# All transposes of a norm-and-convolution kernel on VectorE and DMA, sums on GpSimd, and the order from a list scheduler

## The chip, the cores and the metric

The kernel runs on one core of one Trainium2 chip. The metric is the device time of one execution in microseconds; the time of before is the median of three executions. Every tensor is fp32.

## The reference

Two layers run on x of shape (4, 128, 128, 128): 4 images, 128 channels, 128x128 positions. Cut to what matters:

```python
def _block(x, ...):                                  # tokens = positions, 128 channels each
    t = x.reshape(b, c, h * w).transpose(0, 2, 1)
    t = _ln(t, ln0_g, ln0_b)
    y1 = _ln(t, ln1_g, ln1_b)
    t = t + einsum('btc,oc->bto', sigmoid(y1) * y1, W_out)
    y2 = _ln(t, ln2_g, ln2_b)
    wht = einsum('btc,oc->bto', y2, W_whiten)
    k = square(relu(einsum('btc,hc->bth', wht, W_key)))      # 512 hidden
    kv = einsum('bth,ch->btc', k, W_value)
    r = sigmoid(einsum('btc,oc->bto', wht, W_recep))
    return (t + r * kv).transpose(0, 2, 1).reshape(b, c, h, w)

# layer 0: _gn is a group norm over 4 channels and all positions of an image.
# out1 is _block(inp); out2 is _block on the image with h and w swapped, swapped back.
# _block works on each token alone, so out1 == out2.
x = x + (out1 + out2)(_gn(x))
# layer 1: 3x3 convolution of _gn(x), 128 to 128 channels, a bias, and a gate per channel
x = x + (conv(_gn(x)) + bias) * sigmoid(relu(avg @ se_w1.T) @ se_w2.T)
```

The group norm needs the sums of a whole image before its first token can be worked on. So the convolution of an image can start only when layer 0 of that image has ended.

## The kernel before, in words

**Tiling.** An image has 16384 positions: 8 blocks of 16 rows, or 16 pairs `g` of two chunks `h` of 512 tokens. Layer 0 goes by pairs, the convolution by blocks. Channel layout means 128 channels on the partitions and tokens along the row; token layout means 128 tokens on the partitions and, along the row, four groups of 128 channels.

**Layer 0.** Each step has a short name, which the orders use:

- `u` (`lay`, ACT) applies the group norm in channel layout. `Tu` (`lay_turned`) turns the chunk to token layout by four TensorE transposes through `turned` at L659. `bn0` (DVE, L692) takes the token statistics.
- `nb` (`norm_terms`) makes `rs` and `nb` of a layer norm: small operations on POOL (L704, L705, L722) and a power of -1/2 (L717, POOL).
- `t` (`scaled`, ACT, L666) normalizes; `g` and `b` (POOL, L739, L743) apply gain and shift; `bn1`, `nb`; `z` (ACT, L666) normalizes again; `Tz` turns `z` back to channel layout on TensorE.
- `silu` (ACT), `att` (TensorE, L760) returns to token layout, `T` (DVE, L764) adds it to `t`. `bn2` and `nb2` make the last norm, whose 1/std per token is turned by DVE (`rc`, L772), stored to HBM (`W`, L778, four DMAs) and read back broadcast over the partitions as `R` (L783, two DMAs).
- `tt` turns `t` to channel layout on TensorE. `cp` (DVE, L796) multiplies it with `R` into the input `y2` of the keys; `S` (DVE, L844) adds twice `tt` to x.
- `pk` (4 matmuls, L807), `re` and `sq` (ACT, L811, L817), `kv` (4 matmuls, L834), `pr` (L825), `th` (ACT), `q` (DVE, L850), `x1` (POOL, L854), and `bx`, the statistics for layer 1 (DVE, L860).

**Convolution.** Per block, six products `m0` to `m5` (Winograd along the rows, four output rows from six inputs) of three accumulating matmuls each (L872 to L874), 12 DVE operations ahead of them (`p`, `q`, `v1`...) and 10 after (`a`, `b`, `y0`...), and two ACT evictions. The x of a block stays in SBUF from layer 0 to the end of its convolution (`xp`, 12 buffers of 1 MB).

**Order.** Every engine works in program order. The program order is written out in text lists: `FILL`, `FIRST`, `HANDOVER`, `ORDER`, `BOUND`, `END`. The convolution of image b lies between the pairs of image b+1; the last image's stands at the end. All DMAs of the main part are issued by SP's queue, in that order too. PSUM has eight banks: `h` 2, `kv` 1, `tr` 2, `ut` 2, `conv` 1.

Of the kernel before, what the change touches and what calls it, by code (L numbers as in the profile page):

```python
# [21 lines left out]
LAG = 4  # L22


ORDER = """
    u1:0 Tu1:0 u0:0 x11:3 Tz10:1 Tu0:0 bn01:0 bn00:0 z11:1 bx1:3 v1:1 pr0:2 Tz11:1 q2:1
    silu0:1 p2:1 re00:2 sq00:2 y2:1 ca:1 att0:1 silu1:1 c0:1 pk01:2 nb0:0 d8:1 kv00:2 T0:1
    y0:1 th0:2 t1:0 bn20:1 v3:1 tt1:2 g1:0 re01:2 in0:0 c1:1 cp1:2 e1:1 att1:1 pk02:2 c3:1
    T1:1 bn21:1 pk10:2 c5:1 b1:0 y3:1 re02:2 S1:2 t0:0 nb2:1 e3:1 pk03:2 v2:1 g0:0 b0:0
    re10:2 c2:1 in1:0 a:1 pk12:2 sq01:2 sq10:2 v0a:1 sq02:2 re03:2 sq03:2 re12:2 b:1 kv01:2  # L30
    kv02:2 rc:1 pk13:2 re13:2 v4:1 pk11:2 kv03:2 sq12:2 c4:0 bn11:0 v5a:0 tt0:1 bn10:0 v0b:1
    pr1:2 q0:2 c:0 d:0 re11:2 sq11:2 S0:1 sq13:2 kv10:2 v5b:0 kv11:2 th1:2 kv12:2 kv13:2
    nb1:0 W:1 y1:0 R0:1 z10:0 q:0 cp0:1 pk00:1 R1:1 x10:2 p:0 bx0:2 q1:2
"""


FILL = """
    fetch:16 u1:0 u0:0 Tu1:0 bn01:0 u0:1 Tu0:0 u1:1 bn00:0 sa0:0 in1:16 pw0:0 in0:16
    fetch:17 nb0:0 t1:0 t0:0 Tu0:1 g1:0 bn00:1 b1:0 u1:2 Tu1:1 in1:17 g0:0 u0:2 in0:17
    bn11:0 fetch:18 b0:0 bn01:1 sa0:1 bn10:0 pw0:1 sa1:0 nb0:1 pw1:0 in1:18 t0:1 in0:18  # L40
    nb1:0 fetch:19 t1:1 Tu1:2 g0:1 bn01:2 b0:1 z10:0 Tu0:2 bn00:2 g1:1 z11:0 Tz10:0 b1:1
    in0:19 silu0:0 Tz11:0 bn10:1 nb0:2 u0:3 att0:0 in1:19 silu1:0 bn11:1 fetch:20 u1:3
    att1:0 sa1:1 T0:0 bn20:0 pw1:1 t0:2 T1:0 t1:2 bn21:0 g0:2 sa2:0 Tu0:3 nb1:1 pw2:0 Tu1:3
    in1:20 u1:4 in0:20 z10:1 g1:2 bn00:3 fetch:21 z11:1 bn01:3 nb2:0 b0:2 Tz10:1 rc:0 nb0:3
    W:0 silu0:1 Tz11:1 att0:1 silu1:1 in1:21 bn10:2 R0:0 att1:1 in0:21 b1:2 t0:3 T0:1
    fetch:22 T1:1 tt0:0 t1:3 g0:3 bn11:2 R1:0 tt1:0 Tu1:4 nb1:2 cp0:0 u0:4 bn20:1 u0:5 Tu0:4
    pk02:0 in1:22 S1:0 u1:5 bn01:4 pk00:0 re02:0 pk01:0 re00:0 g1:3 cp1:0 pk03:0 z10:2
    sq00:0 b1:3 bn00:4 pk11:0 re01:0 b0:3 re03:0 pr0:0 in0:22 z11:2 bn21:1 fetch:23 kv00:0
    nb0:4 pk10:0 S0:0 sq01:0 bn10:3 Tz10:2 re11:0 kv01:0 silu0:2 sa2:1 pk12:0 re10:0 bn11:3
    att0:2 sq02:0 pw2:1 sq03:0 kv02:0 T0:2 th0:0 nb2:1 nb1:3 Tz11:2 t1:4 rc:1 kv03:0 sq10:0  # L50
    W:1 pk13:0 q0:0 silu1:2 Tu1:5 in0:23 re12:0 att1:2 bn20:2 t0:4 R0:1 pr1:0 g1:4 bn01:5
    kv10:0 sq11:0 R1:1 x10:0 T1:2 Tu0:5 sq12:0 kv11:0 z10:3 bn00:5 tt1:1 tt0:1 nb0:5 kv12:0
    th1:0 cp0:1 re13:0 pr0:1 sq13:0 cp1:1 pk03:1 z11:3 S1:1 pk00:1 bn21:2 th0:1 kv13:0 g0:4
    S0:1 re00:1 Tz11:3 bx0:0 pk01:1 re03:1 b1:4 sq00:1 silu1:3 pk02:1 b0:4 bn11:4 re01:1
    Tz10:3 att1:3 re02:1 nb2:2 bn10:4 silu0:3 pk12:1 q1:0 pk10:1 re12:1 T1:3 att0:3 sq03:1
    bn21:3 sq01:1 kv00:1 nb1:4 re10:1 pk11:1 sq02:1 rc:2 sq10:1 W:2 pk13:1 re11:1 T0:3
    kv01:1 sq11:1 bn20:3 t1:5 kv02:1 x11:0 R0:2 kv03:1 sq12:1 nb2:3 tt0:2 q0:1 re13:1 R1:2
    pr1:1 bx1:0 t0:5 kv10:1 S0:2 kv11:1 sq13:1 kv12:1 x10:1 z10:4 cp0:2 tt1:2 pk01:2 g0:5
    S1:2 th1:1 pk00:2 cp1:2 re01:2 g1:5 pk03:2 re00:2 rc:3 kv13:1 sq00:2 re03:2 in1:23
    pk02:2 q1:1 pk10:2 bx0:1 x11:1 kv00:2 Tz10:4 bx1:1  # L60
"""
FILL_SLOTS = 6

EARLY = 2

FIRST = """
    u1:0 u0:0 Tu1:0 pk11:4 re02:4 pr0:4 z11:2 Tu0:0 in1:0 re10:4 silu0:2 Tz11:2 sq01:4
    bn01:0 W:3 att0:2 b1:1 sq10:4 bn00:0 R0:3 T0:2 th0:4 silu1:2 re11:4 kv01:4 b0:1 pk12:4
    sq03:4 tt0:3 bn10:1 sq02:4 pk13:4 sq11:4 cp0:3 re12:4 pr1:4 att1:2 th1:4 kv02:4 re13:4
    kv03:4 nb0:0 bn11:1 bn20:2 T1:2 S0:3 pk01:3 pk00:3 pk03:3 bn21:2 tt1:3 t0:0 q0:4 kv10:4  # L70
    nb1:1 sq12:4 kv11:4 re01:3 re00:3 sq13:4 in0:0 nb2:2 S1:3 kv12:4 sq00:3 kv13:4 R1:3
    x10:4 cp1:3 pk02:3 rc:2 q1:4 bx0:4 t1:0 x11:4 g1:0 z10:1 bx1:4 pk10:3 kv00:3 Tz10:1 g0:0
    re03:3
"""
FIRST_SLOTS = 17

ORDER_FROM = 23
HANDOVER = """  # L80
    load load load fetch:32 sq01:13 W:14 z11:15 re02:13 Tz11:15 R0:14 silu0:15 kv01:13 u1:17
    att0:15 R1:14 silu1:15 b0:16 pk11:13 T0:15 re10:13 att1:15 bn20:15 b1:16 u0:17 pk13:13
    re11:13 T1:15 Tu1:17 * bn21:15 tt0:14 re13:13 pr1:13 sq03:13 sq10:13 nb2:15 pr0:13
    sq02:13 bn01:17 u1:18 Tu0:17 pk12:13 bn00:17 sq11:13 kv02:13 th0:13 bn10:16 nb0:17
    sq13:13 tt1:14 kv03:13 th1:13 cp0:14 re12:13 q0:13 pk00:14 u0:18 bn11:16 kv10:13 sq12:13
    re00:14 pk01:14 cp1:14 x10:13 t1:17 S1:14 kv11:13 sq00:14 pk03:14 nb1:16 S0:14 t0:17
    Tu1:18 kv12:13 re01:14 pk12:14 bn01:18 re03:14 Tu0:18 u0:19 pk02:14 bn00:18 g0:17
    kv13:13 z10:16 rc:15 W:15 g1:17 tt0:15 q1:13 pk10:14 sq03:14 S0:15 sq01:14 nb0:18
    kv00:14 * re12:14 kv01:14 * re02:14 R0:15 * re10:14 pr0:14 bx0:13 sq02:14 R1:15 sq10:14
    pk11:14 sq12:14 Tz10:16 th0:14 b0:17 kv02:14 t1:18 kv03:14 x11:13 cp0:15 pk13:14 re11:14  # L90
    bn10:17 b1:17 t0:18 pk00:15 q0:14 pr1:14 bn11:17 sq11:14 x10:14 Tu0:19 * tt1:15 kv10:14
    * * nb1:17 th1:14 * kv11:14 re00:15 * kv12:14 cp1:15 re13:14 bn00:19 silu0:16 pk02:15
    sq13:14 sq00:15 re02:15 kv13:14 g0:18 S1:15 u1:19 pr1:15 q1:14 z11:16 b0:18 att0:16
    bx0:14 pk01:15 x11:14 z10:17 Tu1:19 Tz11:16 g1:18 bn01:19 pk03:15 th1:15 silu1:16
    kv00:15 T0:16 nb0:19 re01:15 bn20:16 pr0:15 z11:17 att1:16 bn10:18 re03:15 in1:32
    Tz11:17 pk10:15 sq01:15 T1:16 b1:18 sq03:15 bn21:16 Tz10:17 kv01:15 re10:15 nb2:16
    sq02:15 sq10:15 pk11:15 silu1:17 bx1:14 kv02:15 th0:15 kv03:15 silu0:17 t0:19 q0:15
    att0:17 rc:16 x10:15 bn11:18 W:16 pk12:15 re11:15 bx1:13 tt0:16 nb1:18 sq11:15 pk13:15
    T0:17 u0:20 bx0:15 t1:19 R0:16 Tu0:20 bn20:17 kv10:15 kv11:15 R1:16 re12:15 S0:16
    re13:15 att1:17 bn00:20 g0:19 sq12:15 sq13:15 kv12:15 g1:19 * kv13:15 cp0:16 u1:20 *  # L100
    b1:19 u1:21 Tu1:20 q1:15 pk01:16 z10:18 bn01:20 x11:15 pk00:16 nb0:20 re01:16 bx1:15
    Tz10:18 pr0:16 re00:16 T1:17 sq00:16 * tt1:16 silu0:18 bn21:17 * th0:16 att0:18 sq01:16
    cp1:16 nb2:17 t0:20 * pk10:16 p:0 bn11:19 pk11:16 t1:20 pk03:16 S1:16 * T0:18 b0:19
    re10:16 kv00:16 * rc:17 re03:16 in0:32 kv01:16 W:17 g1:20 re11:16 bn10:19 Tu1:21 z11:18
    pk02:16 b1:20 bn01:21 pk12:16 R0:17 re02:16 nb1:19 * Tz11:18 bn11:20 sq02:16 tt0:17
    u0:21 kv02:16 fetch:33 S0:17 sq03:16 bn20:18 * Tu0:21 re12:16 R1:17 pk13:16 * sq10:16
    bn00:21 kv03:16 g0:20 silu1:18 cp0:17 pr1:16 z11:19 q0:16 b0:20 att1:18 sq11:16 kv10:16
    * T1:18 sq12:16 nb0:21 tt1:17 * in0:33 re13:16 kv11:16 in1:33 th1:16 pk00:17 S1:17
    fetch:34 sq13:16 * z10:19 kv12:16 * bn10:20 * * re00:17 kv13:16 bn21:18 nb1:20 * Tz10:19
    * t0:21 cp1:17 pk01:17 in0:34 Tz11:19 pk02:17 re01:17 * * silu1:19 pk10:17 * q:0  # L110
    silu0:19 nb2:18 pr0:17 q2:0 sq00:17 att1:19 * re10:17 att0:19 t1:21 T1:19 pk03:17 q1:16
    x10:16 sq01:17 kv00:17 rc:18 bn21:19 re02:17 W:18 g1:21 kv01:17 sq02:17 T0:19 pk12:17
    th0:17 g0:21 in1:34 re03:17 kv02:17 bn20:19 x11:16 R0:18 sq03:17 tt0:18 z10:20 pk11:17
    S0:18 b0:21 kv03:17 * bx0:16 sq10:17 pk13:17 nb2:19 q0:17 re12:17 Tz10:20 * re11:17
    kv10:17 z11:20 cp0:18 pr1:17 * pk00:18 * sq11:17 b1:21 bn10:21 Tz11:20 re13:17 kv11:17
    silu0:20 p2:0 pk02:18 re00:18 v3:0 silu1:20 pk01:18 v1:0 th1:17 rc:19 att1:20 bn11:21
    W:19 re02:18 att0:20 * re01:18 nb1:21 T1:20 c1:0 sq01:18 bn21:20 u0:22 R1:19 T0:20 u1:22
    bn20:20 R0:19 tt0:19 e1:0 Tu1:22 tt1:18 x10:17 sq02:18 bn01:22 c3:0 R1:18 z11:21 nb2:20
    * fetch:35 sq13:17 sq12:17 Tu0:22 pr0:18 sq00:18 bn00:22 e3:0 pk03:18 th0:18 v4:0 nb0:22
# [17 lines left out]
"""  # L137

BOUND_SLOTS = 1, 7
BOUND = """
# [138 lines left out]
def conv_preact_kernel(  # L282
# [17 lines left out]
    se_w2_t: bass.AP,  # L300
    out: bass.AP,
):

# [876 lines left out]
```

## Time and profile before

| What | Value |
|---|---|
| median of 3 runs | 1856.72 us (1855.88 to 1857.11) |
| profiled execution, own time | 1858.43 us |
| its span, first to last instruction | 1856.7 us |
| busy: PE, DVE, ACT, POOL | 97%, 70%, 68%, 53% of the span |
| moved by DMA | 133.44 MB, mean 72 GB/s |
| mean granted TensorE clock | 0.997 |

A page of the profile lists busy time by engine, the chain of work that ended last (followed back from the last instruction, each step to what released it), and groups of instructions with their mean duration and the idle time ahead of them. An fp32 matmul shows as two records, so 512 matmuls are "x1024". The trace can be asked further: for windows of time, for waits by releaser, and for the chain in order of time.

### The profile page before, as it was taken

What the parts mean: (1) busy time and instruction counts of PE and PEld (TensorE: products, weight loads), DVE (VectorE), ACT (ScalarE), POOL (GpSimd) and SP (SyncE); (2) the same over time, 40 slices, a digit from 0 to 9 for tenths busy, and PEclk for the clock granted to TensorE, in tenths of its full rate; (3) what the DMA queues carried; (4) which work ended last, traced back from release to release, by engine and by line L of the source; (5) the groups of instructions that cost most, each with busy time, mean ns of one, the idle gap of its engine ahead of it and who ended that gap; (6) DMA issues with size and microseconds to landing.
All of it is one profiled execution on the core that took longest, in us unless ns stands there. A gap on an engine that the chain in (4) does not pass through costs nothing.

```text
span 1856.7 us, 20165 instructions
## 1 busy us (share of the span) xinstructions
PE 1801.5 (97%) x6096; PEld 944.4 (51%) x6096; DVE 1308.8 (70%) x2540; ACT 1271.1 (68%) x2493; POOL 989.1 (53%) x1047
## 2 busy tenths in 40 slices
PE   3899999999999999999999999999999999999999
PEld 2555555555445555555555555555555555544443
DVE  6766666676667667877667667877766666666987
ACT  2988998898567777777667767777766777753000
POOL 2867677775355555765435555666445556531111
PEclk9999999999999999999999999999999999999999
DMA  6211112121211222222112212211201211111112
GB/s 231 80 58 46 58 65 99 45 71 58 97 57 63 91 79 95 90 80 104 35 68 92 91 48 67 76 63 69 82 16 65 68 58 69 50 40 46 50 68 90
DMA packets 46057, 133.44 MB, mean 72 GB/s; under 512 B 8679, under 2 KB 15102, under 8 KB 38014
## 3 DMA queue, kind: packets, MB, share of 16 engines
q1 hardware_dynamic: 45504, 131.77, 20.6%
q8 instruction: 48, 0.79, 0.2%
q14 instruction: 59, 0.48, 0.1%
q10 hardware_dynamic: 446, 0.40, 0.1%
HBM read 97.14 MB, written 35.00 MB: 71 GB/s over the span
## 4 chain that ended last, share of the span: by engine, by line
PE 89%; DVE 3%; DMA 1%; ACT 1%; POOL 1%; issue 0%; SPq 0%; DVEq 0%; POOLq 0%
PE kv L834 22%; PE pk L807 22%; PE m L872 9%; PE m L873 9%; PE m L874 8%; PE att L760 6%; PE pr L825 6%; PE tt L659 3%; PE z1t L659 3%; PE ut L659 3%; DMA R<-rd 1%; DMA rd<-rrow 1%; DVE v L896 0%; DVE u L606 0%; SPq L778 0%
## 5 line engine op out<-in xcount | busy, mean ns | idle before, releaser
L811 ACT ACTIVATE h<-pk,kbias 128x512 f32<-128x512 f32 x512 | 349.4, 687 | 234.3 <-PE pk L807 223.2
L807 PE MATMUL pk<-y,wk_s 128*128 128x512 f32 x1024 | 502.1, 593 | 2.2 <-DVE y L796 1.2
L834 PE MATMUL kv<-h,wv 128*128 128x512 f32 x1024 | 492.6, 593 | 0.0
L854 POOL TENSOR_TENSOR x<-x,r 128x512 f32<-128x512 f32 x128 | 167.9, 1312 | 275.9 <-DVE r L850 266.0
L834 PEld LDWEIGHTS kv<-h,wv 128*128 128x128 f32 x1024 | 187.1, 190 | 201.8 <-issue 176.0
L817 ACT ACTIVATE h<-h 128x512 f32<-128x512 f32 x480 | 286.5, 629 | 3.4
L807 PEld LDWEIGHTS pk<-y,wk_s 128*128 128x128 f32 x1024 | 183.7, 190 | 183.1 <-issue 153.7
L717 POOL TENSOR_TENSOR rs<-rs,nhalf 128x8 f32<-128x8 f32 x128 | 226.4, 1769 | 4.3 <-DVE nb L705 4.1
L739 POOL TENSOR_TENSOR t<-t,g 128x512 f32<-128x512 f32 x128 | 163.7, 1284 | 101.3 <-ACT t L666 100.9
L666 ACT ACTIVATE t<-ut,nb,rs 128x128 f32<-128x128 f32 x512 | 191.3, 466 | 37.0 <-POOL nb L722 31.2
L666 ACT ACTIVATE z<-t,nb,rs 128x128 f32<-128x128 f32 x512 | 209.3, 491 | 0.0
L872 PE MATMUL m<-v,u 128*128 128x512 f32 x384 | 198.0, 597 | 8.1 <-DVE v L896 4.1
L692 DVE BATCH_NORM_STATS2 st<-t 128x6 f32<-128x256 f32 x512 | 189.8, 418 | 9.5 <-POOL t L743 7.6
L873 PE MATMUL m<-v,u 128*128 128x508 f32 x384 | 195.7, 591 | 0.0
L874 PE MATMUL m<-v,u 128*128 128x508 f32 x384 | 195.0, 589 | 0.0
L743 POOL TENSOR_TENSOR t<-t,b 128x512 f32<-128x512 f32 x128 | 167.5, 1317 | 5.6
L850 DVE SCALAR_TENSOR_TENSOR r<-r,kv 128x512 f32<-128x512 f32 x128 | 87.3, 682 | 110.0 <-PE kv L834 109.5
L704 POOL TENSOR_SCALAR rs<-st 128x8 f32<-128x8 f32 x124 | 41.9, 338 | 209.3 <-DVE st L692 208.0
L764 DVE TENSOR_TENSOR t<-att,t 128x512 f32<-128x512 f32 x128 | 87.9, 687 | 92.0 <-PE att L760 90.7
L760 PEld LDWEIGHTS att<-wo,y 128*128 128x128 f32 x1024 | 131.9, 196 | 31.8 <-issue 25.3
L760 PE MATMUL att<-wo,y 128*128 128x128 f32 x1024 | 138.1, 280 | 1.0 <-DVE t L764 0.6
L825 PE MATMUL pr<-y,wr_s 128*128 128x512 f32 x256 | 130.7, 594 | 0.8 <-DVE h L821 0.6
(146 smaller groups left out, 2352.0 us busy)
## 6 DMA issues: line engine op xcount, KB each, us to landing
R<-rd SPq DMA_DIRECT2D x128, 256.0 KB
x<-in_x SPq DMA_DIRECT2D x31, 1024.0 KB
out<-x SPq DMA_DIRECT2D x31, 1024.0 KB
xs<-in_x SPq DMA_DIRECT2D x48, 512.0 KB
rd<-rrow SPq DMA_DIRECT2D x256, 1.0 KB
u<-raw SPq DMA_DIRECT2D x18, 192.0 KB
raw<-u SPq DMA_DIRECT2D x6, 192.0 KB
x<-in_x SPq DMA_DIRECT2D x2, 512.0 KB
```

Of the source, the lines that this page charges most:

```text
L666: nc.scalar.activation(dst[:, s, :], src[:, s, :], AF.Identity, bias=nb[:, i : i + 1], scale=rs[:, i : i + 1],)
L692: nc.vector.bn_stats(st[:, i : i + 2, :].rearrange("p n f -> p (n f)"), two)
L717: nc.gpsimd.tensor_tensor(rs, rs, nhalf, ALU.pow)
L760: nc.tensor.matmul(att[:, ts(s, P)], y[:, ts(s, P)], wo, start=True, stop=True)
L807: nc.tensor.matmul(pk, wk_s[:, ts(j, P)], S["y2", g, h], start=True, stop=True)
L811: nc.scalar.activation(k, S["pk", g, h, j], AF.Relu, bias=kbias[:, j : j + 1])
L817: nc.scalar.activation(k, k, AF.Square)
L825: nc.tensor.matmul(pr, wr_s, S["y2", g, h], start=True, stop=True)
L834: nc.tensor.matmul(S["kv", g, h], wv[:, j, :], S.pop(("h", g, h, j)), start=(j == 0), stop=(j == NH - 1))
L872: nc.tensor.matmul(pc, u[:, 1], v, start=True, stop=False)
L873: nc.tensor.matmul(pc[:, :, 1:W], u[:, 0], v[:, :, 0 : W - 1], start=False, stop=False)
L874: nc.tensor.matmul(pc[:, :, 0 : W - 1], u[:, 2], v[:, :, 1:W], start=False, stop=True)
```

## The change

The change rewrites the body of the kernel; what is computed stays.

- **Transposes.** No transpose is left on TensorE. For `u`, each block is loaded a second time as `xd` with its rows split so that partition block `a` holds row group `a` (four DMAs on 32 partitions each); after that, one DVE instruction that turns 32x32 blocks gives a chunk in token layout. For `z` and `t`, `to_channels` turns 32x32 blocks on DVE, stores the pair to HBM by four DMAs of 32 partitions and 128 KB, and reads it back by one DMA of 512 KB.
- **Moves.** `cp` and `S` go from DVE to POOL. The small operations of a norm go from POOL to DVE (`e`, `m`); the power stays on POOL (`w`). The factor 2 of `S` is folded into gain, shift and `W_out`.
- **x between the layers** goes through HBM: `xo` stores a block after layer 0, `xc` loads it with its two border rows for the convolution. The statistics of the first image read it once (`xf`) and layer 0 reads it again.
- **R** is one DMA of 512 KB for a pair, in pieces of 1 KB; `W` is one DMA.
- **Squares.** As before, one in four squares per chunk is DVE's in the first image (now to two pairs beyond it), all others ACT's.
- **PSUM**: `Bh` 3, `Bkv` 1, `Btr` 2, `Bconv` 2 banks.
- **Order.** Every step is registered with an engine, costs, a priority, and what it reads and writes. `Plan.order` simulates the five queues, the buffers (`ROOM`), the DMAs (rate 250e3 bytes per us, 8 in flight) and the SBUF port that DVE and POOL share, and picks step by step; the kernel then issues in that order. `SHIFT` moves priorities by kind.

The core of the diff (the lists of before and the parts that only changed their form are left out):

```diff
-ORDER = """
-    u1:0 Tu1:0 u0:0 x11:3 Tz10:1 Tu0:0 bn01:0 bn00:0 z11:1 bx1:3 v1:1 pr0:2 Tz11:1 q2:1
...
+SQUARES = (("DAAA", "DAAA"), ("AAAA", "AAAA"))
+CONV_AT, CONV_STEP = 2.0, 2.0
+LOOK = {'PE': 0.07, 'DVE': 0, 'ACT': 0, 'POOL': 0, 'SP': 0}
+HASTE = 10.307
+Z_BY_DMA, T_BY_DMA = True, True
+CP_ON, S_ON = "POOL", "POOL"
+ROOM = dict(
+    x=3, xd=2, xs=2, ut=3, t=7, z=2, y=2, zd=2, zc=2, td=2, tt=2, R=2, y2=2, h=6, r=2, xc=2, vt=4, v=4,
+    yt=4, uw=9, Bh=3, Bkv=1, Btr=2, Bconv=2, st=6, rs=6, nb=4, four=2, rrow=2, rd=2, zs=2, ts=2,
+)
...
+class Plan:
+    ISSUE, LANDING, RATE, LANES = 0.335, 1.85, 250e3, 8
...
+                    if o["port"]:
+                        if e == "DVE" and pool_port[0] <= r < pool_port[1] - 0.13:
+                            r = pool_port[1] - 0.13
+                        elif e == "POOL" and dve_port[0] <= r < dve_port[1] - 0.13:
+                            r = dve_port[1] - 0.13
...
+                limit = first + LOOK.get(e, 0.0)
+                r, i = min(((r, i) for r, i in picks if r <= limit), key=lambda p: (ops[p[1]]["prio"] + HASTE * (p[0] - first), p[1]))
...
-    def turned(src, tag, name):
-        pt = bank(tag, name).rearrange("p (s c) -> p s c", s=SUB)
-        for s in range(SUB):
-            nc.tensor.transpose(pt[:, s, :], src[:, s, :], ident)
-        return pt
...
+    def load_turned(k):
+        t = ("xd", k)
+        src = rows_of(k).rearrange("(q j) (a r) w -> a j q (r w)", q=SUB, a=SUB)
+        def load(a):
...
+            nc.sync.dma_start(T[t][32 * a : 32 * a + 32], src[a])
...
+            def turn(h=h, r=r):
+                src = T[xd].rearrange("p q (r m i) -> p q r m i", r=PER, i=32)[:, :, r]
+                dst = make(("ut", g, h), "ut").rearrange("p m (q j) -> p q m j", q=SUB)
+                nc.vector.transpose(dst, src)
...
+        def to_channels(name, src, td, tc_, h):
...
+            def turn():
+                dst = T[td][:, :, h].rearrange("p q (m i) -> p m q i", i=32)
+                nc.vector.transpose(dst, T[src].rearrange("p m (q j) -> p m q j", j=32))
...
+            def store(a):
...
+                dst = T[ds_].rearrange("(q j) a h w -> a j q (h w)", j=32)[a]
+                nc.sync.dma_start(dst, T[td][32 * a : 32 * a + 32].rearrange("p q h w -> p q (h w)"))
...
+            def fetch():
+                nc.sync.dma_start(make(tc_, tc_[0]), T[ds_])
...
-        nc.vector.tensor_tensor(y, flat(S["tt", g, h]), S.pop(("R", g, h)), ALU.mult)
+                (nc.gpsimd if eng == G else nc.vector).tensor_tensor(dst, channels(), T["R", g][:, :, h], ALU.mult)
...
-        nc.vector.scalar_tensor_tensor(
-            xs, flat(S["tt", g, h]), 2.0, xs, ALU.mult, ALU.add
-        )
+                (nc.gpsimd if eng == G else nc.vector).tensor_tensor(xs, channels(), xs, ALU.add)
...
+                op(f"e{n}", V, TINY, g, with_eps, both, [(rs, 0)], [(rs, "rs")])
+                op(f"w{n}", G, (1.635, 1.67), g, root, [(rs, 0)], [(rs, 0)])
+                op(f"m{n}", V, TINY, g, shift, [*both, (rs, 0)], [(nb, 0)], [(nb, "nb")])
...
+                nc.sync.dma_start(spill[b][:, kb * BLK_ROWS : (kb + 1) * BLK_ROWS, :], T[xt])
...
+            nc.sync.dma_start(make(xc, "xc")[:, shift : shift + n, :], spill[b][:, lo:hi, :])
...
+        for o in plan.order():
+            o["emit"]()
```

## The prediction

> **What bounds the kernel now.** I read the busy shares first, then the windows of time, then the chain in order of time.
>
> ```profile
> PE 1801.5 (97%) x6096; PEld 944.4 (51%) x6096; DVE 1308.8 (70%) x2540; ACT 1271.1 (68%) x2493; POOL 989.1 (53%) x1047
> ...
> PE 89%; DVE 3%; DMA 1%; ACT 1%; POOL 1%; issue 0%; SPq 0%; DVEq 0%; POOLq 0%
> ```
>
> TensorE (PE) carries 89% of the chain that ended last. The windows (columns: length, then busy time of PE, PEld, DVE, ACT, POOL, clock, DMA share, GB/s) show where it is not alone:
>
> ```profile
> 0.00:20.00 20.00, 6.15 (x12) 2.96 (x12) 11.22 (x19) 3.40 (x11) 2.54 (x13) 1.00 0.92 361
> ...
> 60.00:100.00 40.00, 38.75 (x156) 23.10 (x156) 28.03 (x64) 35.65 (x75) 34.35 (x41) 0.91 0.23 67
> 100.00:200.00 100.00, 100.00 (x377) 55.10 (x376) 66.11 (x132) 90.49 (x181) 66.77 (x76) 1.00 0.20 59
> ...
> 800.00:1000.00 200.00, 199.23 (x678) 104.00 (x677) 144.91 (x276) 143.43 (x281) 106.54 (x109) 1.00 0.21 73
> ```
>
> In the first image PE is full and ACT at 90%; later PE is full and no other engine is over 73%. DMA is a fifth used. The chain between 616 and 625 us gives PE's price per step (start, duration, line, records):
>
> ```profile
> 616.94 0.44 PE z1t L659 x4
> 617.38 0.44 PE ut L659 x4
> 617.82 0.86 PE pr L825 x2
> 618.68 0.44 PE z1t L659 x4
> 619.12 0.89 PE att L760 x8
> 620.01 0.86 PE pk L807 x2
> 620.87 0.86 PE kv L834 x2
> 621.73 0.44 PE tt L659 x4
> 622.16 0.86 PE m L872 x2
> 623.02 0.85 PE m L873 x2
> 623.88 0.85 PE m L874 x2
> ```
>
> A pair in layer 0 costs PE 18 x 0.86 (pk, kv, pr) + 2 x 0.89 (att) + 6 x 0.44 (turns) = 19.9 us. The chain repeats at that pitch in the first image:
>
> ```profile
> 124.49 1.72 PE kv L834 x4
> ...
> 144.36 1.72 PE kv L834 x4
> ...
> 164.22 1.72 PE kv L834 x4
> ```
>
> A product of the convolution is 2.57 us. A pair beside half a block costs 19.9 + 3 x 2.57 = 27.6 us. Whole kernel: 64 x 19.9 + 192 x 2.57 = 1767 us. The profiled execution took 1858.43 us (span 1856.7, 0.1% above the median of 1856.72; I sum against it). The other 91 us are the start (PE is solid from some 63 us, with 15 us of this work done by then), the set-up, and small gaps.
>
> **What the Trainium skill says.** (1) "VectorE: DVE Perf Modes", The three transpose paths: VectorE turns 32x32 blocks only, so HBM must join them, as the change does. The trace has just one small case, rc at 128x32 in 201 ns. (2) "SBUF — State Buffer", Who interferes with whom: a DVE operation with two SBUF inputs and a GpSimd operation that reads SBUF lock each other out for the whole instruction. The trace agrees. The first line is from 600 to 1600 us, the second from 1730 to 1850 us, where POOL is nearly idle:
>
> ```profile
> L896 DVE SCALAR_TENSOR_TENSOR v<-q,p 128x512 f32<-128x512 f32 x36 | 27.4, 760 | 0.1
> L896 DVE SCALAR_TENSOR_TENSOR v<-q,p 128x512 f32<-128x512 f32 x15 | 10.1, 683 | 0.0
> ```
>
> (3) The same page, Door 1: a DMA on 32 partitions reaches half of the 16 ports, measured there at 189 GB/s for 1 MiB. No run here shows such a DMA.
>
> **PE, removed.** All six turns of a pair go: 64 x 6 x 0.44 = 169 us, all on the chain. What is left is 17.26 us a pair in the first image, 24.97 us later, and 1598 us in all. Whether the time follows depends on what comes up beneath.
>
> **DVE, per later pair.** Now 0.73 x 27.6 = 20 us. Added: six turns of 128x512. The nearest rows are whole-tile DVE passes of 680 to 690 ns, which pipeline at about 0.61; I take 0.61 to 0.68, so 3.7 to 4.1 us. Five small norm operations at 0.16 each add 0.8. Removed: cp and S, 4 x 0.68 = 2.7, and the border pieces of v0a, v5a, 0.4. The lock costs the eight two-input operations a mean of 0.1 us now. POOL's reading time rises from 13 to 18 us a pair, so I add 0.5 to 2.5 us. Sum 22 to 24 us: under 25, but not by much.
>
> **POOL.** g, b, x1 at 1.29 (6 of them), cp and S at the same price (4 more), three powers at 1.77: 18.2 us, and 19 to 21 with waits on the lock. In the first image, without the convolution, 10 x 1.28 + 3 x 1.67 = 17.8 us.
>
> **ACT.** Unchanged: 0.905 x 19.87 = 18.0 us a pair in the first image, 19.8 later. Silu now reads SBUF in strides; I cost it at nothing to 0.1 us.
>
> **DMA.** Bytes per later pair: z and t each 0.5 MiB out and in, R, x, xd, xs, xo and out 0.5 each, xc 0.56: 5.56 MiB, 5.8 MB, against about 2.0 MB before. In windows of before, transfers in pieces of 8 KB ran at 361 GB/s with a DMA share of 0.92, and a window of R alone (102.5 to 104 us, pieces of 2 KB) at 253 GB/s with 0.66: 380 to 390 at full share. At half ports, some 190, go zW, tW and xd, 1.57 MB: 8.3 us. The rest, 4.3 MB at 340 to 385: 11 to 12.6 us. So DMA is busy 19 to 21 us of 25, a share near 0.8. In the first image, without xc and out, 4.8 MB: 8.3 + 8.5 to 9.5, some 17 us. If pieces of 1 KB and mixed reads and writes cost more, it is more. SP issues about 17 DMAs a pair at 0.35 us, 6 us: not a limit. But its queue is in order: a zW that waits for a late zD holds up R, xd and xc behind it.
>
> **First image.** PE needs 17.3, ACT 18.0, POOL 17.8, DMA 17, DVE 15 us a pair. Four queues are within 5%, so I take 19.3 (18.0 to 20.5), hardly under the 19.87 of now. The start is longer: before, the first pk comes at 70.4 us. The new path from the group norm's end (33 us) is u 2.8, turn and bn0 2, norm 2.3, t 3, gain and shift 4, bn1 and norm 3, z 3, turn 0.7, out 4, in 3.8 (W and R now take 2.5 and 3.8 us to land), silu, att, T 3, bn2 and power 3, W and R 6.3, cp 1.3: 75 us, and 80 with other pairs in between. Layer 0 of image one ends on PE at 80 + 15 x 19.3 + 17 = 387 us, about where it does now.
>
> **Later images.** 48 pairs. At PE's own pace, 25.0 each. With DVE at 90%, DMA, ACT and POOL near 80%, buffers of two pairs and a fixed order, I allow 4%: 26.0 each, 1248 us. Then the last convolution, 8 x 15.4 = 123 us, and around it the last norm and drain. Now the norm leaves PE idle 5 us at 1700 to 1730; with less left over to fill it and the trip of x through HBM, 10 us. Here xc has two buffers: out (5 us) and the next load (5 us) must fit into the other block's 15.4 us. They do. Total 387 + 1248 + 123 + 10 = **1768 us**, 90 below the profiled execution.
>
> **Rivals.**
> - *The queues fit together nearly perfectly*: 25.2 us a pair and 18.4 in the first image give 373 + 1210 + 133 = 1716. For it: PE is idle under 2% of the later windows now. Against: now every other engine has a quarter of slack.
> - *DMA becomes the bound*, slower. With DMA setting the pace all along, the time is 80 + 133 + (16 x 4.8 + 48 x 5.8) MB / r; it passes 1858 where the mean rate r falls below 216 GB/s. At 205 it is 1946. For it: three kinds of transfer on 32 partitions, 1 KB pieces, everything through one queue; the planner itself reckons with 250. Against: my mean is 5.8 MB / 20 us = 290.
> - *The fixed order stalls PE*: each pair now crosses DVE, SP, HBM and POOL twice, and one late step holds its whole queue. Break-even is 27.6 us a pair, stalls of 10%. At 28.2 the time is 1874.
> - *The change doesn't do what it says*: both DMA switches are on and the branches with TensorE transposes are dead, so I give this nothing.
>
> **How the numbers follow.** Two executions can be told apart here at about 0.2%, 4 us. Chances: the likeliest case (period 25.4 to 27.4) 0.57, the near-perfect fit 0.15, about even 0.03, DMA bound 0.13, stalls over 10% 0.12. So faster 0.72, same 0.03, slower 0.25. The likeliest case alone spans 1735 to 1840. The range goes from 1705, which leaves out 0.05, to 1890, which takes in the nearer half of the slower cases.
>
> **What would show it.** Right: no PE records from a transpose; PE busy near 1640 us at a share of 90 to 95%; DVE turns of 128x512 near 0.65 us; DMA share 0.7 to 0.85 at 230 GB/s; POOL 70%; the pitch of kv near 19 us in the first image, near 26 later. Wrong: a DMA share at 0.95 or more with DVE and ACT waiting for zR and R (the second rival); PE waiting on cp or on ACT's evictions with DMA below 0.8 (the third); DVE turns over 1 us, which would make DVE the bound.

## The result, and the profile after

| | before | after |
|---|---|---|
| median | 1856.3 us (1853.6 to 1857.11) | 1872.94 us (1868.68 to 1876.42) |
| ratio to before | | 1.0091 (95%: 1.0065 to 1.0117) |
| profiled execution, span | 1858.43, 1856.7 us | 1875.05, 1873.3 us |
| mean granted TensorE clock | 0.997 | 0.984 |

The change is **0.9% slower**, where 4.8% faster was forecast. The page of after, busy times, queue and chain by engine:

```profile
PE 1677.0 (90%) x4616; PEld 791.5 (42%) x4616; DVE 1533.4 (82%) x2910; ACT 1282.8 (68%) x2491; POOL 1163.6 (62%) x857
...
q1 hardware_dynamic: 185952, 379.20, 66.9%
...
PE 35%; DVE 27%; DMA 15%; POOL 10%; ACT 7%; issue 4%; SPq 2%; ACTq 0%; DVEq 0%; POOLq 0%
```

The 1536 records of TensorE's turns are gone (56 others, for the group norm, came in). But PE, which carried 89% of the chain, now carries 35%, and no other engine has taken its place: DVE, DMA, POOL and ACT share most of the rest. The windows after, cut where the last `kv` of the first pair, of image 0 and of image 3 ends (length, busy PE, PEld, DVE, ACT, POOL, clock, DMA share, GB/s):

```profile
0.00:131.00 131.00, 44.37 (x143) 28.74 (x144) 88.32 (x190) 73.89 (x161) 70.23 (x67) 0.93 0.74 220
131.00:428.00 297.00, 270.53 (x782) 127.90 (x780) 238.85 (x484) 261.62 (x511) 241.15 (x182) 0.98 0.80 228
428.00:1000.00 572.00, 535.62 (x1498) 252.31 (x1498) 508.21 (x966) 439.10 (x854) 413.34 (x295) 0.99 0.73 223
1000.00:1711.00 711.00, 683.96 (x1868) 320.67 (x1867) 572.61 (x1060) 496.75 (x947) 437.07 (x313) 0.99 0.64 192
1711.00:1873.00 162.00, 142.49 (x330) 61.94 (x328) 125.45 (x214) 11.44 (x20) 1.83 (x2) 0.98 0.35 128
```

In image 0, ACT is at 88%, POOL at 81%, DVE and DMA at 80%, and PE at 91%, where it had been full. Later DVE is at 81 to 89%. TensorE's groups show whom it waits for (busy, mean ns, idle before, releasers):

```profile
L964 PE MATMUL kv<-h,wv 128*128 128x512 f32 x1024 | 528.7, 601 | 22.2 <-DVE r L972 22.2
L926 PE MATMUL pk<-y,wk_s 128*128 128x512 f32 x1024 | 507.5, 609 | 56.0 <-POOL y L909 32.6 <-ACT h L931 15.3 <-DVE rs L713 3.3
...
L868 PE MATMUL att<-wo,y 128*128 128x128 f32 x1024 | 138.7, 281 | 51.4 <-ACT y L848 51.4
```

PE waits for POOL, ACT and DVE in turn. The groups of DVE show a surprise:

```profile
L727 DVE SCALAR_TENSOR_TENSOR nb<-st,rs 128x8 f32<-128x8 f32 x128 | 77.7, 608 | 35.9 <-POOL rs L724 35.8
L713 DVE TENSOR_SCALAR rs<-st 128x8 f32<-128x8 f32 x128 | 58.4, 458 | 1.1
L716 DVE TENSOR_SCALAR four<-st 128x32 f32<-128x32 f32 x64 | 20.6, 321 | 0.5
```

These are the small norm operations that moved from POOL to DVE: 128x8 or 128x32 elements, yet 0.32 to 0.61 us in the mean. The timeline (start, duration) shows why:

```profile
61.73 1.27 POOL L822 TENSOR_TENSOR t<-t,g 128x512 f32<-128x512 f32 x1 [2.25 <-ACT t L756]
62.33 0.71 DVE L713 TENSOR_SCALAR rs<-st 128x8 f32<-128x8 f32 x1
...
64.08 0.16 DVE L713 TENSOR_SCALAR rs<-st 128x8 f32<-128x8 f32 x1
...
64.72 1.27 POOL L822 TENSOR_TENSOR t<-t,g 128x512 f32<-128x512 f32 x1
64.79 1.22 DVE L727 SCALAR_TENSOR_TENSOR nb<-st,rs 128x8 f32<-128x8 f32 x1
```

`rs` starts at 62.33 beside `g` on POOL and ends at 63.04, as `g` does (63.00). At 64.08, beside a power on POOL (63.11 to 64.76) and no pass over a whole tile, the same instruction takes 0.16. `nb` at 64.79 again ends with POOL, at 66.01 beside 65.99. A small operation pays for what is left of the pass next door. Of all 320, 146 took over 0.25 us, and each of these ended 0.02 to 0.19 us after a whole-tile pass on POOL. The time above 0.16 us is 106 us in sum. The page "SBUF — State Buffer" of the Trainium skill, Who interferes with whom, states that `tensor_scalar` too can take the port that DVE shares with GpSimd, and that the one that comes second blocks until the first one's instruction ends. For whole-tile passes the trace agrees. The power is different, though it reads SBUF as well: 37 of the small operations ran beside a power alone, and took 0.13 to 0.21 us, as the undisturbed ones do (0.12 to 0.18); in run 12 there are 95 of them, at 0.12 to 0.18.

### The profile page after: what moved, and what is told of

Read it like the earlier page. It is cut to its first block, busy times and chain, and to the rows that moved or that the text cites. A ratio compares the mean times of both kernels' runs of the same rounds, so it can differ in the third digit from the quotient of the medians.

```text
span 1873.3 us, 18081 instructions
## 1 busy us (share of the span) xinstructions
PE 1677.0 (90%) x4616; PEld 791.5 (42%) x4616; DVE 1533.4 (82%) x2910; ACT 1282.8 (68%) x2491; POOL 1163.6 (62%) x857
## 3 DMA queue, kind: packets, MB, share of 16 engines
q1 hardware_dynamic: 185952, 379.20, 66.9%
## 4 chain that ended last, share of the span: by engine, by line
PE 35%; DVE 27%; DMA 15%; POOL 10%; ACT 7%; issue 4%; SPq 2%; ACTq 0%; DVEq 0%; POOLq 0%
PE pk L926 9%; PE kv L964 8%; DVE st L700 5%; PE m L1084 4%; PE m L1085 4%; PE m L1086 4%; DMA tt<-ts 3%; PE att L868 3%; DMA xd<-in_x 2%; PE pr L951 2%; DMA ts<-td 2%; ACT z L756 2%; POOL rs L724 2%; DMA R<-rd 2%; POOL four L724 2%
## 5 line engine op out<-in xcount | busy, mean ns | idle before, releaser
L964 PE MATMUL kv<-h,wv 128*128 128x512 f32 x1024 | 528.7, 601 | 22.2 <-DVE r L972 22.2
L931 ACT ACTIVATE h<-pk,kbias 128x512 f32<-128x512 f32 x512 | 339.5, 680 | 97.3 <-PE pk L926 81.7
L926 PEld LDWEIGHTS pk<-y,wk_s 128*128 128x128 f32 x1024 | 191.9, 193 | 319.5 <-issue 189.2
L909 POOL TENSOR_TENSOR y<-tt,R 128x512 f32<-128x512 f32 x128 | 166.8, 1313 | 134.1 <-PE pr L951 57.5
L756 ACT ACTIVATE t<-ut,nb,rs 128x128 f32<-128x128 f32 x512 | 209.3, 486 | 54.8 <-DVE nb L727 38.5
L1084 PE MATMUL m<-v,uw 128*128 128x512 f32 x384 | 200.0, 602 | 25.2 <-DVE v L1063 14.4
L1085 PE MATMUL m<-v,uw 128*128 128x508 f32 x384 | 197.1, 595 | 0.0
L1086 PE MATMUL m<-v,uw 128*128 128x508 f32 x384 | 195.8, 592 | 0.0
L919 POOL TENSOR_TENSOR x<-tt,x 128x512 f32<-128x512 f32 x128 | 168.5, 1331 | 29.4 <-DMA tt<-ts 29.4
L724 POOL TENSOR_TENSOR four<-four,nhalf 128x8 f32<-128x8 f32 x64 | 111.0, 1734 | 63.4 <-DVE four L716 54.2
L956 ACT ACTIVATE r<-pr,rbias 128x512 f32<-128x512 f32 x128 | 86.0, 681 | 70.5 <-PE pr L951 70.4
```

Of the source, the lines that this page charges most:

```text
L724: nc.gpsimd.tensor_tensor(r, r, nhalf, ALU.pow)
L756: nc.scalar.activation(dst[:, s, :], src[:, s, :], AF.Identity, bias=nb[:, i : i + 1], scale=rs[:, i : i + 1])
L926: nc.tensor.matmul(make(pk, "Bh"), wk_s[:, ts(j, P)], T[y2], start=True, stop=True)
L931: nc.scalar.activation(make(hh, "h"), T[pk], AF.Relu, bias=kbias[:, j : j + 1])
L964: nc.tensor.matmul(T[kv], wv[:, j, :], T["h", g, h, j], start=(j == 0), stop=(j == NH - 1))
L1084: nc.tensor.matmul(pc, u[:, 1], vv, start=True, stop=False)
```

## The experiments

Two theories at first. **Operations**: the loss lies in the work itself, on DVE, POOL, the queue or PE's clock. **Order**: the work would fit, but the order is made from a table of costs that lacks something. In the code, the two-input operations of the convolution carry `port=True`, so `Plan` lets them wait for POOL. The small operations `e0`, `e1`, `e2`, `m0`, `m1` don't.

In runs 1 to 3, 5 to 7, 9 and 10 the operations stand in the order of after, but for the four loads that run 3 moves; only what an entry issues is changed. Runs 4, 8, 11 and 12 to 14 have an order made anew.

**1. The small operations back on POOL.**

```diff
-                nc.vector.tensor_scalar(make(rs, "rs"), T[st][:, :, 2], ...)
+                nc.gpsimd.tensor_scalar(make(rs, "rs"), T[st][:, :, 2], ...)
```

(`nb` and `four` likewise, `nb` in two instructions.)

> The five small norm operations of a pair (L713, L716, L727) are issued on POOL instead of DVE, everything in the same program order. Theory 1 (the lock between DVE and POOL): their 157 us on DVE, of which 106 us are waits for POOL, leave DVE and POOL gains 110 us; DVE was late, so 1815 to 1845 us. Theory 2 (the round trips through HBM set the pace): within 12 us of the change's 1873, or slower because POOL is fuller.

Measured: 1927.93 us, ratio 1.0385 (1.0365 to 1.0405). No lock is left for them, and DVE has less to do, yet it is 55 us slower than after: POOL's time is as dear as DVE's. Theory 1, as put there, falls.

**2. Stores and loads over all partitions.** The four stores of `zW` and `tW` and the loads of `xd` take a column block of 128 partitions each instead of 32 partitions; the data land elsewhere, so the output is another one.

```diff
-                nc.sync.dma_start(dst, T[td][32 * a : 32 * a + 32]...)
+                nc.sync.dma_start(T[ds_][:, a]..., T[td][:, a]...)
```

> Same program order; the four stores of a turned pair and the four loads of xd each take a quarter of the row of all 128 partitions instead of the whole row of 32 partitions, so bytes, piece sizes and number of DMAs stay and the blocks are not put together rightly (the output is another one). Theory 2 (DMA sets the pace, most of all its half-port transfers): the DMA share falls from 0.67 to about 0.5 and the time to below 1840 us. Theory 1 (the lock): the share falls, the time stays within 15 us of 1873.

Measured: 1851.88 us, ratio 0.9994 (0.9979 to 1.001), 21 us under after. Its page:

```profile
q1 hardware_dynamic: 185952, 379.20, 62.5%
```

66.9% of 1873.3 us were 1253 us of all 16 engines; 62.5% of its 1862.0 us are 1164. The 101 MB on 32 partitions cost 89 us more than at this page's mean rate of 326 GB/s (379.2 MB in 1164 us). If all else ran alike, they ran at some 253 GB/s, not at the 190 of the prediction: an estimate. The queue has a part in the loss, but a small one.

**3. The first four `xd` ahead of the sixth `xf`.**

```diff
+        first = [o for o in made if o["name"] == "xd"][:4]
+        for o in made[:at] + first + made[at:]:
```

> Only the four loads of the first block's xd are moved ahead in the order, before the sixth of the eight loads for the statistics. Theory 3 (the longer start is lost for good): the first u begins at about 35 us instead of 42.9 and the whole is 7 to 9 us shorter, near 1865. Rival: other things (xs, raw, POOL's gain and shift) set the first keys' time, and the whole moves by less than 4 us.

Measured: 1873.9 us, 1.0105 (1.0088 to 1.0122): nothing gained. `xd` came earlier, but the group norm's `nb` came later, at 41.9 us instead of 40.8, and the first `u` still starts after both.

**4. The lock told to the planner**, with `port=True` on the five small operations and `w`; the offsets `SHIFT` stay, and the order is made anew.

> No operation moves; the planner is told that the five small norm operations and the power share the port between DVE and POOL (port=True), and makes another order. Theory 1a (the order is wrong because the plan did not know of these waits): a gain of 20 to 50 us, 1825 to 1855. Theory 1b (the waits themselves cost, whoever knows of them): 1855 to 1885, since the other constants were tuned to the old plan. Theory 2 (DMA): 1865 to 1885.

Measured: 1919.1 us, 1.0345 (1.0328 to 1.0363), 46 us slower than after. The small operations wait less in its trace (54 us above 0.16 us instead of 106), so a smaller wait alone doesn't make a fast order. The planner's own reckoning of this order was long already, 1849 us. Part of that is `w`: here the planner lets the power wait for the port as well, and after's trace shows no such wait. Without it, and with the offsets kept, its reckoning ends at 1805 us; no run shows what the chip takes for that order.

**5 and 6. `cp`, then `S`, on VectorE.**

```diff
-                (nc.gpsimd if eng == G else nc.vector).tensor_tensor(dst, channels(), T["R", g][:, :, h], ALU.mult)
+                nc.vector.tensor_tensor(dst, channels(), T["R", g][:, :, h], ALU.mult)
```

> Edit: the product cp (y2 = tt*R) is issued on VectorE instead of GpSimd, at the same place of the same order; 128 passes. GpSimd loses 128 x 1.31 = 168 us of work, VectorE gains 128 x some 0.70 = 90 us (73 us at its pipelined pace). Theory 1, the path through GpSimd and its lock set the loss (PE waits some 51 us on y from GpSimd; small VectorE operations wait some 106 us for GpSimd): the step falls from 1.31 to 0.70 us, L713 and L727 fall toward 0.3 us; 10 to 35 us faster than the changed kernel (1838 to 1863). Theory 2, VectorE is the bound of the later images (85 to 92% busy there): 73 to 90 us more on it, 20 to 60 us slower (1893 to 1933). Theory 3, TensorE's own pace and the granted clock carry the later images: within 8 us of the changed kernel.

> Edit: the sum S (x + tt) is issued on VectorE instead of GpSimd, at the same place of the same order; 128 passes. It is off the path to the next matmul: only x1, the output's statistics and the free buffers wait for it. GpSimd loses 168 us, VectorE gains 73 to 90 us. Theory 1, GpSimd's load and lock: cp, g, b and the powers behind S start earlier, 5 to 25 us faster than the changed kernel (1848 to 1868). Theory 2, VectorE is the bound: 20 to 60 us slower (1893 to 1933). Theory 3, TensorE's own pace: within 8 us.

Measured: 1921.36 us, 1.0367 (1.0329 to 1.0406), and 1912.67 us, 1.0309 (1.0286 to 1.0332): 48 and 40 us slower than after. Some 150 us less on POOL don't pay for 128 passes more on DVE (109 us with `cp`; 57 us net in its busy time, since other waits fall). TensorE's wait for `q` on DVE doubles with `cp` there:

```profile
L964 PE MATMUL kv<-h,wv 128*128 128x512 f32 x1024 | 539.4, 612 | 45.8 <-DVE r L972 45.7
```

**7. Epsilon on ScalarE.** The same additions took 0.29 to 0.36 us there all through the run, so they don't wait for POOL's passes.

```diff
-                nc.vector.tensor_scalar(make(rs, "rs"), T[st][:, :, 2], (C if n == 0 else 4 * C) * LN_EPS, None, ALU.add)
+                nc.scalar.activation(make(rs, "rs"), T[st][:, :, 2], AF.Identity, bias=eps[:, n : n + 1], scale=1.0)
```

> Edit: the small operations that add epsilon (L713, 128 of them, and L716, 64) are issued on ScalarE as Identity with a bias column instead of on VectorE, at the same place of the same order. [...]VectorE loses 58 + 21 = 79 us, ScalarE gains 192 x some 0.2 = 38 us. Theory 1 (lock) and theory 2 (VectorE the bound) both give 15 to 40 us faster than the changed kernel (1833 to 1858). Theory 3 gives no change within 8 us. Theory 4, ScalarE's queue is what is late (90% busy in the first image, PE waits 47 us on h and 18 on r): slower by 5 to 30 us.

Measured: 1861.08 us, 1.0036 (1.0023 to 1.0048), 12 us under after, a little less than the 15 expected at least. DVE's busy time falls by 54 us.

**8. The turn of `z` back on TensorE**, `Z_BY_DMA = False`.

> Edit: only the turn of z goes back to TensorE (Z_BY_DMA = False), t keeps its way through HBM, and the order is made anew by the kernel's own planner. VectorE loses 128 x 0.70 = 89 us, the queue loses a third of its traffic (z out and in, 128 MiB... 64 pairs x 1 MiB = 67 MB), TensorE gains 128 x 0.44 = 56 us. Each pair crosses HBM once fewer, so the start is some 12 us shorter. Theory 1 or 2 (VectorE and its lock set the later pace): 20 to 60 us faster than the changed kernel. Theory 3 (TensorE's own pace): some 56 - 12 = 44 us slower. The planner's own reckoning rises from 1744 to 1790 us (+46), so an order made anew accounts for theory 3's number as well.

Measured: 1897.84 us, 1.0234 (1.0216 to 1.0252), 25 us slower than after. DVE loses 72 us and DMA 67 MB, and PE gains 61. It lies between the theories, and the new order hides which: no verdict.

**9. Full partitions with the right output, and epsilon on ScalarE.** For each column block one DMA: 128 partitions of SBUF against DRAM rows in two steps, 4 by 32 (shown for the stores; the loads of `xd` likewise).

```diff
-                dst = T[ds_].rearrange("(q j) a h w -> a j q (h w)", j=32)[a]
+                dst = T[ds_][32 * a : 32 * a + 32].rearrange("j a h w -> a j (h w)")
```

> Edit, all at the same places of the same order: (a) the four stores of a turned pair and the four loads of xd are cut by the column block q instead of by the row block a, so that each touches all 128 partitions of SBUF and moves the same bytes in pieces of the same size to the same places; (b) the small epsilon operations L713 and L716 run on ScalarE as in the run eps_act. Theory 1: two independent reliefs add, -21 us (transfers over full ports, from full_ports) and -12 us (VectorE, from eps_act): some 1840 us, 0.8% faster than the kernel before. Rival: both relieve the same wait and share it: 1850 to 1856. Rival 2: with pieces of 1 KB scattered over 512 rows per transfer the queue is no faster than in quarters of 32 partitions: 1861, as eps_act alone.

Measured: 2172.27 us, 1.1716 (1.1698 to 1.1733). All three expectations were wrong. Its window from 332 to 340 us, with loads of `xd` on the way:

```profile
332.00:340.00 8.00, 4.44 (x8) 1.59 (x8) 6.19 (x15) 5.85 (x12) 4.55 (x4) 0.74 0.27 97
```

The DMA share is 0.27, near a quarter, at 97 GB/s. The skill's page "DMA: Bandwidth & Descriptors", Rules for kernel authors, states that an outermost dimension below 16 confines a transfer to as many engines, here 4. The share agrees. So the gain of run 2 is not to be had in this way.

**10. Without `b`.** The addition of b0 on POOL is left out.

> Edit: the addition of the row b0 on GpSimd (128 passes of 1.33 us) is left out, everything else at the same place of the same order. This leaves out the shift of the first normalisation, so the output is another one. GpSimd loses 170 us, VectorE's own instructions stay as they are, the start is 1.3 to 2.7 us shorter. Theory 1, the load of GpSimd is a cause in itself (small_pool, which adds 125 us to GpSimd and takes some 160 from VectorE, was 52 us slower): 25 to 60 us faster than the changed kernel (1813 to 1848), with L713, L716 and L727 nearer to 0.3 us. Theory 2, only VectorE's own instructions count: 0 to 10 us faster.

Measured: 1845.38 us, 0.9942 (0.9919 to 0.9965), 28 us under after, for 163 us less on POOL. DVE's own instructions are the same, but its busy time falls by 39 us, 29 of them in the small operations: the lock.

Runs 1, 5, 6, 7 and 10 agree on one thing: 54 to 163 us of busy time on either engine move the end by 12 to 55. Neither engine sets the time alone, and none of these operations explains the loss. What is left to try is the order.

**11. Run 9 with two banks for `kv` and one for `att`**, the order made anew.

> Edit: the run qsplit_eps with two PSUM banks for kv and one for att (Bkv=2, Btr=1 instead of 1 and 2), order made anew by the kernel's own planner. In the changed kernel TensorE waits some 50 us for q on VectorE to free the single bank of kv, and the two banks Btr, which held TensorE's transposes before, now serve att alone. Theory A: that wait goes and half of it is gained: 10 to 30 us faster than qsplit_eps. Theory B: it is VectorE's lateness that shows there, and the wait moves to pk and att: within 15 us of it either way. Theory C: the order made anew costs more than it brings, since the offsets were set for the old buffers, and att on one bank waits for T on VectorE: 20 to 60 us slower.

Measured: 2225.46 us, 1.1989 (1.1949 to 1.2029), 53 us slower than run 9, as theory C had it. But banks and order changed together, on top of the slow transfers of run 9: inconclusive.

**The order by itself.** `Plan` can be held to a given order and asked when it ends, by its own costs, once without and once with the wait of the five small operations (reckoned, not measured, and for all but runs 12 to 14 reckoned afterwards):

| order and operations | without | with | measured median |
|---|---|---|---|
| after | 1744 | 1818 | 1873 |
| 4, old offsets, wait of the power too | 1848 | 1850 | 1919 |
| 5, `cp` on DVE | 1811 | 1858 | 1921 |
| 6, `S` on DVE | 1806 | 1852 | 1913 |
| 7, epsilon on ACT | 1769 | 1805 | 1861 |
| 8, `z` on PE | 1790 | 1862 | 1898 |
| 10, without `b` | 1747 | 1786 | 1845 |
| 12, order with the wait | 1758 | 1757 | 1828 |
| 13, order with the wait, three reliefs | 1751 | 1750 | 1823 |
| 14, order without the wait | 1754 | 1829 | 1868 |

Of 12 to 14 more below. Without the wait, the reckoning has 7 and 10 slower than after, which is wrong. With it, it has them 13 and 32 us faster (measured 12 and 28) and 5 and 6 40 and 34 us slower (measured 48 and 40). It has run 4 32 us slower (measured 46). It is poor on run 1, where no small operation is left to wait: 1839, 21 slower, measured 55. So the planner believed in 1744 us for an order that its own rule, applied to the small operations too, puts at 1818: 74 of the 129 us between plan and chip.

**12. The order alone.** All operations as in after. The planner is told of the wait (without `w`), and its offsets are searched anew for that.

```diff
-                op(f"m{n}", V, TINY, g, shift, [*both, (rs, 0)], [(nb, 0)], [(nb, "nb")])
+                op(f"m{n}", V, TINY, g, shift, [*both, (rs, 0)], [(nb, 0)], [(nb, "nb")], True)
```

> Edit: every operation of the changed kernel stays as it is, on its engine and with its buffers. Only the order changes: the planner is told that the small operations e0, e1, e2, m0 and m1 on VectorE wait for GpSimd (port=True), and its offsets (SHIFT, HASTE, LOOK, BACKLOG) are set anew for those costs. Reckoned with the same costs, the changed kernel's order ends at 1818 us (it was made for 1744, without the lock) and the new one at 1757. Theory A, the loss is the order, which was made without the lock and leaves every queue late in turn: some 40 to 60 us faster than the changed kernel, 1813 to 1833. Theory B, the loss is in the operations (their work, the lock, the transfers, the clock), whatever their order: within 15 us of the changed kernel (1858 to 1888). Theory C, a new order misses as plan_lock's did: some 1919.

Measured: **1827.75 us**, 0.9852 (0.983 to 0.9873): 45 us under after, 29 under before. Page and windows:

```profile
PE 1668.3 (91%) x4616; PEld 796.0 (44%) x4616; DVE 1461.5 (80%) x2910; ACT 1290.0 (71%) x2491; POOL 1162.4 (64%) x857
...
PE 54%; DVE 16%; ACT 10%; DMA 9%; POOL 8%; issue 2%; SPq 1%; DVEq 0%; POOLq 0%; ACTq 0%
```

```profile
428.00:1000.00 572.00, 559.46 (x1604) 269.71 (x1605) 520.24 (x1061) 472.92 (x925) 442.96 (x318) 0.99 0.77 239
```

The same 2910 instructions keep DVE busy for 72 us less. PE is at 98% from 428 to 1000 us, where it was at 94%, and carries 54% of the chain instead of 35%. The small operations:

```profile
L731 DVE SCALAR_TENSOR_TENSOR nb<-st,rs 128x8 f32<-128x8 f32 x128 | 54.3, 425 | 18.0 <-POOL rs L728 17.7
L717 DVE TENSOR_SCALAR rs<-st 128x8 f32<-128x8 f32 x128 | 35.4, 278 | 0.7
L720 DVE TENSOR_SCALAR four<-st 128x32 f32<-128x32 f32 x64 | 13.9, 221 | 0.2
```

Their time above 0.16 us is 53 us, half of after's 106, and ACT's `z` waits 18 us for `nb` instead of 79.

**13. The order with the single reliefs**: epsilon on ACT, `S` on DVE, two banks for `kv` and one for `att`, searched anew.

> Edit: as retune, and besides epsilon on ScalarE (L713, L716), S on VectorE, two banks for kv and one for att; offsets set anew for that, with these costs told to the planner. Its reckoning ends at 1750 us, 6 below retune's. Theory A, the order is the loss: some 1805 to 1828, 1.5 to 2.7% under the kernel before. Theory B, the operations are the loss: e7's 12 us are gained and S on VectorE costs up to its 40: 1860 to 1900.

Measured: **1823.06 us**, 0.9819 (0.9798 to 0.984), the lowest median here, though its lead of 5 us on run 12 is within the spread of the two. `S` on DVE, 40 us slower in the old order, comes here with two reliefs and an order made for it; what it costs by itself isn't known.

**14. A control**: offsets searched in the same way with the old costs.

> Edit: a control for e12_retune. Every operation as in the changed kernel; the offsets (SHIFT, HASTE, LOOK, BACKLOG) are found by the same kind of search from a lock-aware starting point, but with the planner's old costs, in which the small operations don't wait for GpSimd. Its reckoning ends at 1754 us without the lock (e12_retune's order: 1758) and at 1829 with it (e12_retune's: 1757). Theory A, what e12_retune gained is an order that bears the lock: this one is no better than the changed kernel, 1865 to 1900. Theory B, any other order would have gained, and the lock is beside the point: within 15 us of e12_retune, 1815 to 1843.

Measured: 1868.11 us, 1.0075 (1.0046 to 1.0104). Its small operations:

```profile
L731 DVE SCALAR_TENSOR_TENSOR nb<-st,rs 128x8 f32<-128x8 f32 x128 | 82.7, 648 | 31.1 <-POOL rs L728 31.0
L717 DVE TENSOR_SCALAR rs<-st 128x8 f32<-128x8 f32 x128 | 57.8, 452 | 1.0
```

They wait as in after (648 and 452 ns beside 608 and 458). A new order is not enough; one that bears the wait is 40 us better. This is one control, and run 4 shows that an order made with the wait can also be bad, so the exact share is not known.

## Why the prediction was wrong, point by point

**By its own sum.** It set the ends of the windows at 97, 387, 1635 and 1768 us. After has 131, 428, 1711 and 1873.

| term | forecast | after | off by | run 12 | run 14 |
|---|---|---|---|---|---|
| to the last `kv` of the first pair | 97 | 131 | +34 | 128 | 127 |
| 15 pairs of image 0 | 290 (19.3 each) | 297 (19.8) | +7 | 298 | 296 |
| 48 later pairs | 1248 (26.0) | 1283 (26.7) | +35 | 1217 (25.4) | 1258 (26.2) |
| from there to the end | 133 | 162 | +29 | 182 | 180 |
| sum | 1768 | 1873 | +105 | 1825 | 1861 |

The order explains some 45 of the 105 us, which is what run 12 gains with the same operations. The rest lies in the start and the end.

**The step that failed: "a fixed order, I allow 4%: 26.0 each".** I summed each engine's work, compared shares, and left 1 us a pair for all waits. The pitch came to 26.7. With an order that bears the lock, the same operations run at 25.4, under the forecast. Not all of that step down is gain: 805 matmul records of the convolution stand in these pairs in run 12, 835 in after, and the missing five products, 13 us, stand at the end. Run 14 has the same split as run 12, and its pitch is 26.2: 41 us more in the 48 pairs for an order made without the lock.

**What was left out of it: "Five small norm operations at 0.16 each add 0.8".** That is the duration of an undisturbed one. They take 157 us in all, or 2.45 us a pair. Of the lock the prediction said that it "costs the eight two-input operations"; it read the rule as one for two inputs and whole tiles. The skill's page names `tensor_scalar`, and `nb` has two inputs in SBUF as well. In DVE's sum this did no harm: the 0.5 to 2.5 us put in for the lock took it up, by luck. It failed as a wait. The small ones stand in the chain of a norm: ACT's `z` waited 79 us for `nb`. And a planner that doesn't know them sets every later step too early.

**The rival that came nearest.** *The fixed order stalls PE* described what happened, and its sign came: PE waits for `cp` (`y` on POOL) and for ACT's evictions, with the DMA share below 0.8 in the later windows. But it got a chance of 0.12, and that its 1874 us is almost the result is luck: its pitch of 28.2 us is not what came, and the rest is in start and end. The prediction also gave its break-even as 27.6 us a pair; by its own sum it is (1858 - 387 - 133) / 48 = 27.9.

**The start, +34.** The path was worked out from the group norm's end at 33 us, as before. In after it ends at 40.9: its last statistics come 4.9 us later, and the chain behind them takes 3.4 us more. The DMA share is 0.93 or more from 10 to 43 us, since the first `xd` and `x` are loaded beside `xf`. Then the chain of waits has (start, duration):

```profile
28.28 14.43 DMA xd<-in_x
...
73.31 3.74 DMA zs<-zd
77.07 6.01 DMA zc<-zs
...
96.10 6.90 DMA R<-rd
...
107.19 2.93 PE pk L926 x3
```

From `u` at 42.9 to `pk` at 107.2 are 64 us, where I had 47. Known terms are `zc` (6.0, not 3.8) and `R` (6.9, not 3.8), at DMA shares of 0.89 (77 to 83 us) and 0.91 (96 to 103); the rest is other pairs' work in between. Run 3 shows that `xd` alone is not the cause. The orders of runs 4, 12, 13 and 14, each made anew, have 126 to 133 us, so none of these orders takes this start away. Run 8, where `z` doesn't cross HBM, has 115.

**The end, +29.** The forecast had 8 blocks of 15.4 us and 10 us around them. But before, too, took 151 us there, not 133:

```profile
1705.00:1856.00 151.00, 142.44 (x334) 62.87 (x334) 126.64 (x227) 11.68 (x20) 26.80 (x18) 0.99 0.20 74
```

In after, 317 records of products stand behind the last `kv`, 136 us instead of 123, and 26 us are not products. The end is longer still in run 12, with its five products more. What the last norm alone cost wasn't tried.

**Right:** the turns of DVE (694 to 701 ns, forecast near 0.65 us), DVE at 22 to 24 us a later pair (1081 us in 48 pairs, 22.5), PE's share (90%), the pitch of image 0 within 0.5 us. **DMA:** 0.64 to 0.80 busy, near the forecast's 0.8; that transfers on 32 partitions weren't faster cost 21 us (run 2).

**What stays open.** What made the start and the end long is only known in part. With the wait told to it, the reckoning still ends 36 to 73 us early (55 for after), and 89 in run 1. The granted clock is part of that: after's mean of 0.984 misses 30 us of full clock, before's 0.997 misses 6. But run 13 has 0.995 and gains just 5 us on run 12 with 0.981, so this is no simple sum. And only after's order was searched anew; what a search would bring to before's, which is written out by hand, wasn't tried.

## What to carry to other kernels

When work moves between VectorE and GpSimd, price its small operations beside the neighbour's passes, not alone: here 146 of 320 instructions of 128x8 or 128x32 elements waited, and took up to 1.4 us instead of 0.16. When several queues stand at 80% or more, the sum of the work isn't enough and the order counts, so a scheduler's table must hold the waits too, and its offsets must be set for them: the same instructions took 1873 us with a table without the lock, 1828 with it and offsets searched for it, and 1919 with a table that had a wait too many and the old offsets. Before blaming an operation, hold the order and move that one alone; then hold the operations and move the order.

## What was unexpected of the hardware

**The clock falls after an idle PE.** TensorE was idle for 4.45 us up to 245.14 us. The windows after that:

```profile
236.00:245.00 9.00, 3.70 (x8) 1.44 (x8) 8.66 (x19) 4.71 (x10) 9.00 (x7) 0.95 0.82 236
245.00:246.00 1.00, 0.86 (x1) 0.50 (x2) 1.00 (x3) 0.88 (x3) 1.00 (x2) 0.50 1.03 281
246.00:250.00 4.00, 4.00 (x6) 1.69 (x5) 4.00 (x10) 2.07 (x3) 4.00 (x4) 0.50 1.06 251
...
250.00:252.00 2.00, 2.00 (x5) 0.72 (x4) 0.93 (x5) 1.33 (x3) 1.40 (x2) 0.75 0.73 196
252.00:254.00 2.00, 2.00 (x6) 0.94 (x5) 0.42 (x1) 2.00 (x5) 2.00 (x3) 1.00 0.95 307
```

The granted clock is 0.50 for some 6 us, and a stall is paid for twice. The skill's page "TensorE: Matmul & The Clock Gate", Part 1, states half rate after an idle window of about 3.4 us and full rate after a busy one. The trace agrees: half after 4.45 us idle, full again by 252 us. The prediction had no such term, and no run took it away by itself.

**Four engines.** A transfer that reaches all 128 partitions, but is written as 4 by 32 on its other side, moved at 97 GB/s (run 9). As four transfers of 32 partitions the same bytes went at some 253, by the estimate under run 2.
